# A change of order at the beginning of a perceiver layer: two PSUM copies and one weight transfer

## The chip, the core and the metric

The kernel runs on one core of a Trainium2 chip. The metric is the device time of one execution in microseconds (us), and "the time" of a kernel is the median of its runs. Engines are named as in the profile: PE is TensorE (matmuls; PEld its weight loads), DVE is VectorE, ACT is ScalarE, POOL is GpSimd, and SP is the engine whose queue issues nearly all transfers.

## The reference

One layer of a perceiver. A latent x of 128 rows and 512 columns attends over a context of 12544 rows with 16 heads of 128; then follow a linear attention with decay and a feed-forward part with quantized weights. Nearly all the work is in the first part:

```python
def _L0_xattn_ref(inputs_q, inputs_kv, Wq, Wk, Wv, Wo):
    q = (inputs_q @ Wq).reshape(b, sq, H, HD) * (1.0 / np.sqrt(HD))
    k = (inputs_kv @ Wk).reshape(b, skv, H, HD)
    v = (inputs_kv @ Wv).reshape(b, skv, H, HD)
    scores = jnp.einsum('bqhd,bkhd->bhqk', q, k)
    attn = jax.nn.softmax(scores, axis=-1)
    ctx = jnp.einsum('bhqk,bkhd->bqhd', attn, v).reshape(b, sq, H * HD)
    return ctx @ Wo
...
x = x + _L0_xattn_ref(_layernorm(x, axis=-1), ctx_2048, ...)
x = x + _L0_attn_ref(_layernorm(x, axis=-1), ...)
x = x + _L0_ffn_ref(_layernorm(x, axis=-1), ...)
```

All of it is float32.

## The kernel before

**The algebra.** The kernel never forms the keys. It multiplies each head's query with that head's part of Wk, which gives for 16 heads and 128 rows a matrix of 512 by 2048, and multiplies the context with that matrix to get the scores. The 12544 context rows are taken in 98 pairs of 128; the 2048 score columns in two halves, f = 0 and f = 1. One unit (i, f) is a context pair times a half. Scores go to DRAM; a second pass reads them back, takes the exponential, and multiplies it with the context (L469).

**A unit.** A unit (`unit`, L180) is computed as a block product with seven products instead of eight (p1 to p7), from sums of the context blocks (S1 to S4) and sums of the matrix blocks (T1 to T4). To keep float32 accuracy each operand is split into a high part, a rounding cast made by ScalarE, and a low part, the rest, made by VectorE, and each product is six matmuls of 128x512 (L190), each sum of which lies in one PSUM tile `ps`. ScalarE copies p1 out (L225, `p1s`), VectorE adds the others up (L219: U2, U3, c22, c21, c12), and keeps a running maximum (L237).

**The beginning.** It builds the matrix. The weights of the heads are taken in eight pairs, numbered h2 = 0 to 7 ("the fifth pair" is h2 = 4). For each pair:

- `load_w` (L280) names two transfers of 512 KB, Wq's part (`wq`) and Wk's part (`wk`); `begin` (L298) issues them on SP's queue. `load_ct` (L151) issues a transfer of a context pair, 512 KB too.
- q: `project_q` (L337), 16 matmuls at L344, into a PSUM tile `pq`; needs `wq`.
- qT: `scaled` (L354), ScalarE scales and copies it out (L356).
- k: `project_k` (L358), 16 matmuls at L364, into a PSUM tile `pk` of 128 x 1024 f32; needs qT and `wk`.
- ca and cb: `leave` (L382), two copies by ScalarE of the halves of `pk` into the matrix blocks (L384). Both wait for the whole of k.

The PSUM pool of the beginning, `ps_pro` (L277), has two tiles of each name, so two pairs' `pk` at a time. A third can be written only when both copies of one of them are done.

**The order.** The sums and casts of the matrix blocks stand between these steps: `hB111` is the high part of block B11 for f = 1 (ScalarE, L409), `lB111` its low part (VectorE, L398), `T11` the sum T1 for f = 1 (VectorE, L398), S00 to S23 the sums of the first three context pairs (L163 to L166), `hi0` and `lo0` the split of the first (L171, L176). All of them, and the first four units (u00 to u11, of which `u00p1` is the product p1 of the first), are issued in an order written out by hand in one text, `plan` (L266), and each engine keeps that order for its own instructions. At `u00p1` the pool `ps_pro` is closed and `ps_s`, with eight PSUM tiles, is opened in the same memory; with `reuse_waits="tile"` a tile of it waits only for those old tiles that it lies on. From the third context pair on the order is not written out, but planned by the framework.

**The transfers.** They are issued on SP's queue in this order: x, wq0, wq1, wk0, wk1, wq2, wk2, the first context pair, wq3, wk3 (L304 to L306), then wq4, wk4, the second context pair, and wq5, wk5, wq6, wk6, wq7, wk7 (L331, L333).

Of the kernel before, what the change touches and what calls it, by code (L numbers as in the profile page):

```python
# [33 lines left out]
def tile_perceiver_layer(  # L34
# [116 lines left out]
    def load_ct(i):  # L151
        if i == 1:
            raw = spare(B22, [P, 8, 2, P])
        else:
            raw = ctp.tile([P, 8, 2, P], F32, tag="raw", name="ctr", bufs=1)
        nc.sync.dma_start(out=raw[:, A11:, :, :], in_=cT[i])
        return raw
# [22 lines left out]
    def unit(i, f, place):  # L180
# [83 lines left out]


    plan = """  # L266
        q0 q1 qT0 k0 qT1 k1 c0a c0b q2 c1b hB210 lB210 q3 qT2 c1a hB110 S01 S00 k2 S02 qT3 lB110 S03 k3 c2b c2a hi0
        S11 q4 S10 S12 S13 c3b lo0 ct2 c3a q5 qT4 hB220 T10 k4 qT5 hi1 T30 k5 T20 hT10 lo1 hT30 q6 c4b c5a T40 q7 qT6
        hT20 lB220 c5b k6 lT20 qT7 hT40 lT30 k7 c6a lT40 c6b c4a lT10 u00p1 c7a hB111 u00p6 c7b lB111 hB221 u00p7 T11
        u00p1s u00U2 hT11 u00p5 u00U3 hB211 u00p4 u00c22 T21 u00p2 u00c21 hT21 T31 u00p3 u00c11 lT21 hT31 u10p1 u00c12  # L270
        lT31 u10p6 u10p1s lB221 u10p7 u10U2 u10p5 u10U3 S20 u10p4 u10c22 lB211 u10p2 T41 u10p3 u10c21 hT41 lT11 u10c11
        u01p1 lT41 u01p6 u01p1s u10c12 u00m2 u01p7 u01U2 u01p5 u01U3 S22 u01p4 u01c22 S21 S23 u01p2 u01c21 u10m1 u01p3
        u01c11 u10m2 u11p1 hi2 u01c12 u01m2 u11p6 u11p1s lo2 u11p7 u11U2 u11p5 u11U3 u11p4 u11c22 u11p2 u11c21 u11m1
        u11p3 u11c11 u11c12 u11m2
    """
    pro = ExitStack()
    ps_pro = pro.enter_context(tc.tile_pool(name="ps_pro", bufs=2, space=PSUM))  # L277
# [2 lines left out]
    def load_w(h2):  # L280

        hs = slice(h2 * 256, (h2 + 1) * 256)
        room = {2: B11, 3: B21, 5: T3, 6: T1}
        if h2 in room:
            both = spare(room[h2], [P, 2, 1024])
            wq = both[:, 0, :].rearrange("p (c e) -> p c e", c=NC)
            wk = both[:, 1, :].rearrange("p (h d) -> p h d", h=2)
        else:
            if h2 == 7:
                wq = mxp.tile([P, NC, 256], F32, tag="mx1", name="wq")  # L290
            else:
                wq = ctp.tile([P, NC, 256], F32, tag="hi", name="wq")
            wk = ctp.tile([P, 2, D], F32, tag="lo", name="wk")
        first = [(wq, x_wq[:, hs].rearrange("(c p) e -> p c e", p=P))]
        first.append((wk, x_wkT[hs, :].rearrange("(h p) d -> p h d", p=P)))
        return wq, wk, first

    def begin(*loads):  # L298
        for to, given in loads:
            nc.sync.dma_start(out=to, in_=given)  # L300

    keep_warm(ps_pro, 9)
    ws = [load_w(h2) for h2 in range(4)]
    begin(ws[0][2][0], ws[1][2][0], ws[0][2][1], ws[1][2][1], *ws[2][2])  # L304
    raws[0] = load_ct(0)
    begin(*ws[3][2])  # L306
    xn = mxp.tile([P, D], F32, tag="mx1", name="xn")
    xnT = tmp.tile([P, NC, P], F32, tag="u3", name="xnT")
    st = small.tile([P, 1, 6], F32, tag="bn", name="st")
# [860 lines left out]
```

## Time and profile before

| what | us |
|---|---|
| median of 3 runs | 2129.59 (2127.59 to 2129.66) |
| the profiled execution | 2127.83 |
| its span in the profile | 2126.1 |
| TensorE busy, 0 to 10 | 7.66 |
| 10 to 20 | 9.04 |
| 20 to 30 | 10.00 |
| 30 to 40 | 8.67 |
| 40 to 50 | 9.27 |
| 50 to 2060 | 2010.00 |
| 2060 to 2126 | 58.03 |

The span runs from the first to the last instruction of one execution, and the profiled execution is a little longer than it. Times in a timeline are counted from the span's start. The two big loops (the scores to 973 us, the second pass to 2039 us) keep TensorE busy without a gap, at the full granted clock (1.00 in all stretches); what isn't busy lies in the first 50 us and in the last 66.

The transfers of the beginning, by issue and by landing (us, from the view of the transfers):

| transfer | issued | from issue to landing |
|---|---|---|
| wk2 | 3.87 | 10.2 |
| first context pair | 4.74 | 10.6 |
| wq3 | 5.98 | 10.9 |
| wk3 | 6.75 | 11.4 |
| wq4 | 9.14 | 10.6 |
| wk4 | 12.47 | 8.6 |
| second context pair | 12.89 | 9.5 |
| wq5 | 13.40 | 10.4 |
| wk5 | 14.05 | 11.1 |

### The profile page before, as it was taken

The page shows a single profiled execution, that of the slowest core. Times are in us where ns is not written, and L with a number is a line of the kernel's source. Part 1 is how long each engine was busy: PE and PEld are TensorE (multiplying, and loading weights), DVE is VectorE, ACT ScalarE, POOL GpSimd, SP SyncE. Part 2 cuts the span into 40 slices and gives each one's busy share as a digit, 9 for nine tenths or more (in the row PEclk, how much of TensorE's full clock was granted, in tenths as well). Part 3 has the DMA queues.
Part 4 walks back from the last instruction along what each step waited for, and adds up shares of the span by engine and source line. Part 5 has one row for each costly group of instructions (what it writes and reads, how often), then busy time and mean ns, then how long its engine had stood idle before and what let it go on. Part 6 is the DMA issues. An engine that isn't in the chain of part 4 may idle for free.

```text
span 2126.1 us, 23916 instructions
## 1 busy us (share of the span) xinstructions
PE 2112.7 (99%) x9591; PEld 1745.2 (82%) x9595; DVE 1646.7 (77%) x1827; ACT 754.2 (35%) x846; POOL 25.7 (1%) x15
## 2 busy tenths in 40 slices
PE   8999999999999999999999999999999999999998
PEld 7888888888888888888888888888888888888885
DVE  6877777777777777778897888887788777777745
ACT  6222122211222122214444444444544444444424
POOL 0000000000000000000000000000010000000010
PEclk9999999999999999999999999999999999999999
DMA  5333333333333333336664454553444434444460
GB/s 207 135 140 127 149 141 137 139 129 149 134 144 137 130 149 129 149 151 216 216 238 150 181 179 168 174 202 143 149 149 149 148 142 140 145 142 146 149 230 6
DMA packets 70767, 326.22 MB, mean 153 GB/s; under 512 B 7265, under 2 KB 11617, under 8 KB 45185
## 3 DMA queue, kind: packets, MB, share of 16 engines
q1 hardware_dynamic: 70512, 324.57, 41.4%
q8 instruction: 75, 1.23, 0.2%
q14 instruction: 36, 0.29, 0.1%
q10 hardware_dynamic: 144, 0.13, 0.0%
HBM read 221.65 MB, written 103.02 MB: 153 GB/s over the span
## 4 chain that ended last, share of the span: by engine, by line
PE 98%; DVE 1%; DMA 1%; ACT 0%; SPq 0%; issue 0%; DVEq 0%; ACTq 0%
PE pu L469 50%; PE ps L190 44%; PE pc L742 1%; PE po L763 1%; PE pk L364 1%; DMA kq<-in_x_wq_dram 1%; PE pp L853 0%; PE pq L344 0%; PE po L906 0%; PE pv L876 0%; SPq L300 0%; DVE uT L1057 0%; DVE st L1031 0%; PE pp L932 0%; ACT kq L409 0%
## 5 line engine op out<-in xcount | busy, mean ns | idle before, releaser
L190 PE MATMUL ps<-kq,cth 128*128 128x512 f32 x2744 | 844.5, 389 | 0.0
L469 PE MATMUL pu<-ph,cl 128*128 128x512 f32 x1568 | 610.0, 389 | 0.0
L469 PE MATMUL pu<-pl,ch 128*128 128x512 f32 x1568 | 610.0, 389 | 0.0
L469 PE MATMUL pu<-ph,ch 128*128 128x512 f32 x1568 | 610.0, 389 | 0.0
L190 PEld LDWEIGHTS ps<-kq,cth 128*128 128x128 f32 x2744 | 515.2, 188 | 106.6
L190 PE MATMUL ps<-kq,ctl 128*128 128x512 f32 x1344 | 522.8, 389 | 0.0
L523 ACT CAST ph<-si 128x1024 fp32r<-128x1024 f32 x194 | 203.9, 1051 | 491.9 <-PE pu L469 491.7
L469 PEld LDWEIGHTS pu<-pl,ch 128*128 128x128 f32 x1568 | 294.4, 188 | 61.2
L469 PEld LDWEIGHTS pu<-ph,cl 128*128 128x128 f32 x1568 | 294.4, 188 | 60.9
L469 PEld LDWEIGHTS pu<-ph,ch 128*128 128x128 f32 x1568 | 294.4, 188 | 60.9
L219 DVE TENSOR_TENSOR so<-ps,u 128x512 f32<-128x512 f32 x294 | 202.7, 690 | 134.9 <-PE ps L190 130.5
L190 PEld LDWEIGHTS ps<-kq,ctl 128*128 128x128 f32 x1344 | 252.3, 188 | 52.4
L511 DVE TENSOR_TENSOR cl<-cr,ch 128x1024 fp32r<-128x1024 f32 x98 | 120.2, 1227 | 204.8 <-ACT ch L505 204.8
L254 ACT COPY so<-ps 128x512 f32<-128x512 f32 x98 | 57.6, 588 | 577.6 <-PE ps L190 577.6
L528 DVE TENSOR_TENSOR pl<-si,ph 128x1024 fp32r<-128x1024 f32 x194 | 242.4, 1250 | 1.0 <-ACT ph L523 1.0
L237 DVE TENSOR_TENSOR mx<-mx,so 128x1024 f32<-128x1024 f32 x190 | 232.2, 1222 | 6.7
L517 DVE TENSOR_TENSOR si<-si,mb 128x1024 f32<-128x1024 f32 x194 | 235.7, 1215 | 0.0
L536 DVE TENSOR_TENSOR lsum<-lsum,si 128x1024 f32<-128x1024 f32 x192 | 233.8, 1218 | 0.0
L518 ACT ACTIVATE si<-si 128x1024 f32<-128x1024 f32 x194 | 205.4, 1059 | 60.4 <-DVE si L517 60.4
L505 ACT CAST ch<-cr 128x1024 fp32r<-128x1024 f32 x98 | 102.3, 1044 | 0.0
L176 DVE TENSOR_TENSOR ctl<-ctr,cth 128x1792 fp32r<-128x1792 f32 x47 | 94.9, 2019 | 0.7 <-ACT cth L171 0.7
L171 ACT CAST cth<-ctr 128x1792 fp32r<-128x1792 f32 x48 | 81.7, 1703 | 37.5 <-PE ps L190 35.5
(224 smaller groups left out, 757.8 us busy)
## 6 DMA issues: line engine op xcount, KB each, us to landing
sc<-so SPq DMA_DIRECT2D x98, 1024.0 KB, 3.8
si<-sc SPq DMA_DIRECT2D x97, 1024.0 KB, 5.0
cr<-in_c_dram SPq DMA_DIRECT2D x98, 512.0 KB, 3.5
ctr<-in_cT_dram SPq DMA_DIRECT2D x48, 512.0 KB, 3.5
kq<-in_w1T_dram SPq DMA_DIRECT2D x16, 512.0 KB, 4.3
kq<-in_w2T_dram SPq DMA_DIRECT2D x16, 512.0 KB, 5.0
kq<-in_x_wv_dram SPq DMA_DIRECT2D x3, 1024.0 KB, 5.2
kq<-in_x_wo_dram SPq DMA_DIRECT2D x3, 1024.0 KB, 7.3
```

Source lines behind the costliest of these rows:

```text
L176: return lo, nc.vector.tensor_tensor(lo, raw[:, :7, :, :], hi, ALU.subtract)
L190: nc.tensor.matmul(ps, lhsT=lt[:, a, cc, :], rhs=right(f, b, part)[:, cc, :], start=(first and n == 0), stop=(n == 5), skip_group_check=True,)
L219: place(nc.vector.tensor_tensor(to, t[p], t[q], ALU.add))
L237: place(nc.vector.tensor_tensor(mx[f], mx[f], t["so"][:, j, :], ALU.max))
L469: nc.tensor.matmul(pu[b][cc], lhsT=lt[:, j, cs], rhs=rt[:, bs], start=(first and n == 0), stop=(last and n == 2))
L505: seq(nc.scalar.copy(ctx_hi[f, i], ctx_raw[f, i]))
L511: seq(nc.vector.tensor_tensor(ctx_lo[f, i], ctx_raw[f, i], ctx_hi[f, i], ALU.subtract))
L517: seq(nc.vector.tensor_tensor(exps[k], exps[k], mb[f], ALU.subtract))
L518: seq(nc.scalar.activation(exps[k], exps[k], AF.Exp))
L523: seq(nc.scalar.copy(high[k], exps[k]))
L528: seq(nc.vector.tensor_tensor(low[k], exps[k], high[k], ALU.subtract))
L536: seq(nc.vector.tensor_tensor(lsum[f], lsum[f], exps[k], ALU.add))
```

## The change

It moves three things and adds or removes none.

1. In the plan, `c4a` (the fifth pair's second copy) goes from behind `c6b` to ahead of `c6a`, directly behind `k7`.
2. In the plan, `c7b` (the last copy) goes from behind `hB111 u00p6` to directly behind `c7a`. On ScalarE it passes one cast, `hB111`.
3. `wq3` is issued ahead of the first context pair and not behind it.

All other lines of the plan are the same words in the same order, with other line breaks. The core of the diff:

```diff
-        hT20 lB220 c5b k6 lT20 qT7 hT40 lT30 k7 c6a lT40 c6b c4a lT10 u00p1 c7a hB111 u00p6 c7b lB111 hB221 u00p7 T11
-        u00p1s u00U2 hT11 u00p5 u00U3 hB211 u00p4 u00c22 T21 u00p2 u00c21 hT21 T31 u00p3 u00c11 lT21 hT31 u10p1 u00c12
...
+        T40 q7 qT6 hT20 lB220 c5b k6 lT20 qT7 hT40 lT30 k7 c4a c6a lT40 c6b lT10 u00p1 c7a c7b hB111 u00p6 lB111
+        hB221 u00p7 T11 u00p1s u00U2 hT11 u00p5 u00U3 hB211 u00p4 u00c22 T21 u00p2 u00c21 hT21 T31 u00p3 u00c11
...
     keep_warm(ps_pro, 9)
     ws = [load_w(h2) for h2 in range(4)]
-    begin(ws[0][2][0], ws[1][2][0], ws[0][2][1], ws[1][2][1], *ws[2][2])
+    begin(ws[0][2][0], ws[1][2][0], ws[0][2][1], ws[1][2][1], *ws[2][2], ws[3][2][0])
     raws[0] = load_ct(0)
-    begin(*ws[3][2])
+    begin(ws[3][2][1])
```

More of the change, by code (lines that the diff above doesn't have):

```diff
@@ L266, in tile_perceiver_layer @@
     plan = """
-        q0 q1 qT0 k0 qT1 k1 c0a c0b q2 c1b hB210 lB210 q3 qT2 c1a hB110 S01 S00 k2 S02 qT3 lB110 S03 k3 c2b c2a hi0
-        S11 q4 S10 S12 S13 c3b lo0 ct2 c3a q5 qT4 hB220 T10 k4 qT5 hi1 T30 k5 T20 hT10 lo1 hT30 q6 c4b c5a T40 q7 qT6
-        hT20 lB220 c5b k6 lT20 qT7 hT40 lT30 k7 c6a lT40 c6b c4a lT10 u00p1 c7a hB111 u00p6 c7b lB111 hB221 u00p7 T11
-        u00p1s u00U2 hT11 u00p5 u00U3 hB211 u00p4 u00c22 T21 u00p2 u00c21 hT21 T31 u00p3 u00c11 lT21 hT31 u10p1 u00c12
[L271 to L274, printed above, removed]
+        q0 q1 qT0 k0 qT1 k1 c0a c0b q2 c1b hB210 lB210 q3 qT2 c1a hB110 S01 S00 k2 S02 qT3 lB110 S03 k3 c2b c2a
+        hi0 S11 q4 S10 S12 S13 c3b lo0 ct2 c3a q5 qT4 hB220 T10 k4 qT5 hi1 T30 k5 T20 hT10 lo1 hT30 q6 c4b c5a
+        T40 q7 qT6 hT20 lB220 c5b k6 lT20 qT7 hT40 lT30 k7 c4a c6a lT40 c6b lT10 u00p1 c7a c7b hB111 u00p6 lB111
+        hB221 u00p7 T11 u00p1s u00U2 hT11 u00p5 u00U3 hB211 u00p4 u00c22 T21 u00p2 u00c21 hT21 T31 u00p3 u00c11
+        lT21 hT31 u10p1 u00c12 lT31 u10p6 u10p1s lB221 u10p7 u10U2 u10p5 u10U3 S20 u10p4 u10c22 lB211 u10p2 T41
+        u10p3 u10c21 hT41 lT11 u10c11 u01p1 lT41 u01p6 u01p1s u10c12 u00m2 u01p7 u01U2 u01p5 u01U3 S22 u01p4
+        u01c22 S21 S23 u01p2 u01c21 u10m1 u01p3 u01c11 u10m2 u11p1 hi2 u01c12 u01m2 u11p6 u11p1s lo2 u11p7 u11U2
+        u11p5 u11U3 u11p4 u11c22 u11p2 u11c21 u11m1 u11p3 u11c11 u11c12 u11m2
     """
```

## The prediction

> **What bounds the kernel now.** I read the busy shares first, then the chain of work that ended last, then the waits of TensorE alone, and last the timeline of the first 50 us.
>
> ```profile
> PE 2112.7 (99%) x9591; PEld 1745.2 (82%) x9595; DVE 1646.7 (77%) x1827; ACT 754.2 (35%) x846; POOL 25.7 (1%) x15
> PE 98%; DVE 1%; DMA 1%; ACT 0%; SPq 0%; issue 0%; DVEq 0%; ACTq 0%
> ```
>
> TensorE is busy for 2112.7 of 2126.1 us. So only the 13.4 us in which it stands still can be won, and the table of stretches finds none of them between 50 and 2060 us. The two product lines of the chain run at one rate in both halves (L190: 931.89 us for 4110, 0.2267 each; L469: 1066.24 us for 4704, 0.2267). An edit in the beginning is worth the idle time that it takes from TensorE there, and no more. TensorE's own waits, those of the beginning:
>
> ```profile
> PE pk L364 <- ACT kq L384: 1.2, 1, 1.2
> PE pq L344 <- DMA kq<-in_x_wq_dram: 1.0, 1, 1.0
> PE ps L190 <- ACT kq L384: 0.7, 1, 0.7
> PE pk L364 <- ACT b L384: 0.2, 1, 0.2
> ```
>
> And where they lie (TensorE's timeline, then ScalarE's; start, duration, in brackets the idle time before):
>
> ```profile
> 14.06 1.95 PE L344 MATMUL pq<-xnT,kq 128*128 128x128 f32 x16
> 16.98 2.02 PE L344 MATMUL pq<-xnT,kq 128*128 128x128 f32 x16 [0.96 <-DMA kq<-in_x_wq_dram]
> ...
> 24.20 1.95 PE L344 MATMUL pq<-xnT,kq 128*128 128x128 f32 x16
> ...
> 33.46 2.05 PE L364 MATMUL pk<-qT,kq 128*128 128x128 f32 x16 [0.17 <-ACT b L384]
> 36.67 2.05 PE L364 MATMUL pk<-qT,wk 128*128 128x128 f32 x16 [1.16 <-ACT kq L384]
> ...
> 40.84 0.50 PE L190 MATMUL ps<-kq,mb 128*128 128x512 f32 x1 [0.73 <-ACT kq L384]
> ```
> ```profile
> 33.67 1.04 ACT L409 CAST kq<-b 128x1024 fp32r<-128x1024 f32 x1
> 35.55 1.07 ACT L384 COPY kq<-pk 128x512 f32<-128x512 f32 x2 [0.84 <-PE pk L364]
> 36.51 0.61 ACT L384 COPY b<-pk 128x512 f32<-128x512 f32 x1
> 38.76 0.59 ACT L384 COPY kq<-pk 128x512 f32<-128x512 f32 x1 [1.65 <-PE pk L364]
> 39.24 1.05 ACT L409 CAST kq<-b 128x1024 fp32r<-128x1024 f32 x1
> 40.19 0.59 ACT L384 COPY kq<-pk 128x512 f32<-128x512 f32 x1
> ```
>
> The reader is to see three stalls, one for each of the three edits. q3 (16.98) waits for the transfer of its weights. k7 (36.67) starts 0.05 us after the two copies c6a and c6b end (35.55 + 1.07 = 36.62), while c4a, put behind them, runs from 36.51: so k7 took the place that k6 left, since k4's was held until c4a. u00p6 (40.84) starts 0.06 us after c7b ends (40.19 + 0.59 = 40.78), which stood behind the cast hB111 (39.24).
>
> [...] the transfers of SP's queue landed one after the other, 1.3 to 1.5 us apart, while the stretch from 2 to 30 us moved 360 GB/s at full DMA share. [...] I count landings (issue plus time to landing), not issues.
>
> **The change part by part.**
>
> *The transfer.* Issued at 4.74, the first context pair landed 10.6 us later, at 15.34; wq3, issued at 5.98, landed 10.86 later, at 16.84, so 1.50 after it. Swapped, wq3 lands near 15.4 to 15.6 and the context pair at 16.84; both issues (0.72 and 1.20 us on SP) keep their two places together, and wk3 and all behind it stay. q2 ends at 14.06 + 1.95 = 16.01, so q3 finds its weights there and its 0.96 us of waiting goes. The context pair's first reader is VectorE's sum at 17.10, behind a subtraction that ends at 17.18 whatever happens; 16.84 is 0.26 earlier, so that is hidden. If it came later than that, the four sums would shift by as much, and their reader, the cast at 21.78, still has 2 us behind their end (19.79).
>
> What is late next is wq5. It was issued at 13.40 and took 10.4 us: it lands at 23.80, its place in the queue unchanged. q5 started at 24.20; 0.96 earlier would be 23.24, but it can't start before 23.80 + 0.14 (q3's own distance from landing, 16.98 - 16.84) = 23.94. So of 0.96 us only 24.20 - 23.94 = 0.26 is left. Bounds: 0.1, if starting from rest costs the 0.07 by which q3's group (2.02) is longer than the others (1.95) and a little more; 0.96, if wq5 lands earlier than I think. I take 0.26. wq6 and wq7 landed at 26.7 and 29.55, at least 1.6 us ahead of their matmuls.
>
> *c4a ahead of c6a.* On ScalarE c4a now follows hT40, which ends at 33.67 + 1.04 = 34.71, and fills the 0.84 us in which ScalarE waited for k6; its 0.61 us end at about 35.3, before k6 ends (33.46 + 2.05 = 35.51). k4's place is then free, k7 follows k6 at once, and its 1.16 us go (all these times less the 0.26). Cover: 0.2 us; if it is gone, k7 waits by so much. c6a and c6b start no later than before. Behind them only VectorE's T-sums wait, after 38. Bounds for this edit: 0, if k7 is still given k6's place, and 1.35, the idle time of the weight loads there. I take 1.16.
>
> *c7b ahead of hB111.* Counted from k7's start, c7a comes 2.09 later (38.76 - 36.67), c7b then ends 1.07 after that, as the pair c6a and c6b did: 3.16. u00p1 starts 1.81 after k7 and lasts to about 3.25 (six matmuls, the first at 38.48, the last begun at 39.72). So even if u00p6 lies in k7's banks, c7b is done when its turn comes, and if k7 has moved into k4's banks it waits for nothing: the 0.73 us go. The price is that hB111 is 0.59 us later behind its copies; its reader, a subtraction on VectorE, and T11 behind it then start 1.0 us sooner than before and not 2.15. That is hidden: the first sum that TensorE needs back, c22, follows them and would be at about 43.1, just as its matmuls end (45.21 - 2.15 = 43.06), and TensorE came for it only 1.83 us after its end (45.94 to 47.77).
>
> *Sum.* 0.26 + 1.16 + 0.73 = 2.15 us of the profiled execution: its 2127.83 (a span of 2126.1 and 1.7 around it) becomes 2125.7. The median of the runs shown, 2129.59, lies 1.76 above that execution; the same difference from it gives 2127.4, 0.10% less.
>
> **Rivals.**
> 1. wq5 doesn't bind, and all three stalls go whole: 0.96 + 1.16 + 0.73 = 2.85, so 2126.7. For it: nothing in the trace but the uncertainty of a landing by some tenths; against: the queue is full up to 30 us.
> 2. The second edit does nothing: k7 still takes k6's place. Then 0.26 + 0.73, 2128.6. Against: c4a is over before c6a can begin.
> 3. u00p1 draws one of k7's new banks. Before it didn't wait, so its bank was not among those read by c7a or c7b; k4's pair is not excluded by that, as c4a ended at 37.12. It would then wait from 1.81 to 3.21 after k7's start, 1.40: 2.15 - 1.40 = 0.75 gained, 2128.8.
> 4. Slower than before: from the third context pair on the order is not written out but planned, and a beginning shortened by 2 us could plan VectorE's maxima (1.22 each, L237) ahead of c22. In the loop c22 ended 1.83 us before TensorE came for it (93.54 to 95.37), once only 0.78 (85.07 to 85.85). Two maxima ahead, 2.44, leave a stall of 0.61 in the unit. It decides from the fourth such unit on (2.44 against 2.15 gained); in each second of 192 units it costs 58.6, about 2186. For it: VectorE is busy for 19.03 of 20 us from 60 to 80. Against: every part of the beginning moves by nearly the same 2 us, so the plan's relations stay.
>
> **How the numbers follow.** Chances: forecast 0.60, first rival 0.10, second 0.11, third 0.11, fourth 0.08. The three runs shown spread by 2.07 us, and 0.2% (4.3 us) is about what a measurement of this kernel tells from no change. The forecast and the first rival pass that bound only with some 2 us of luck from the spread, about a quarter of their 0.70: faster 0.18. The fourth is slower: 0.08. The rest, 0.74, stays within. The range goes from 2125.0 (the level of the profiled execution, 2127.83, less the 2.85 of the first rival) to 2129.9 (the third rival and half the spread), which leaves out the fourth and a tenth more.
>
> **What would show it.** After: q3 without idle time; a new wait of 0.5 to 0.8 us of a later q on its weights' transfer near 23.9; k7 right behind k6 near 35.2; u00p1 near 37.0 and u00p6 near 38.5 without idle time; the chain's first long piece of L190 beginning 2.15 earlier, and the products still at 0.2267 us each with no idle time to 2030. I would be wrong if q5 doesn't wait, if k7 still waits for c6b, or if TensorE idles anywhere after 50 us.

## The result, and the profile after

| | median us | runs | range |
|---|---|---|---|
| before | 2129.03 | 22 | 2127.59 to 2129.96 |
| after | 2126.13 | 22 | 2124.84 to 2128.18 |

The ratio is 0.9987, with a 95% interval from 0.9981 to 0.9993: 2.9 us less, and by the interval between 1.5 and 4.0. The forecast was 2127.4 (2.15 less, 0.10%), the range 2125.0 to 2129.9. Of the 1.3 us between forecast and result 0.56 lies in the starting point, for the three runs of before known then had a median of 2129.59, and the rest in the gain. The profiled execution of after took 2127.29 us, with a span of 2125.6; why it lies above the median is shown below.

TensorE's waits in the beginning, after (what waited for what: us in total, times, longest):

```profile
PE pq L344 <- DMA kq<-in_x_wq_dram: 0.9, 1, 0.9
PE pq L344 <- DMA wq<-in_x_wq_dram: 0.9, 1, 0.9
```

The two waits for copies (1.2 and 0.7 before) are no longer in the list. A wait of some q for its weights still is, and a second one has come. TensorE's timeline says which, and ScalarE's what made room (start, duration, in brackets the idle time before):

```profile
14.83 3.74 PE L344 MATMUL pq<-xnT,kq 128*128 128x128 f32 x32
...
24.79 2.02 PE L344 MATMUL pq<-xnT,kq 128*128 128x128 f32 x16 [0.86 <-DMA kq<-in_x_wq_dram]
...
34.12 2.05 PE L364 MATMUL pk<-qT,kq 128*128 128x128 f32 x16 [0.17 <-ACT b L384]
36.01 1.95 PE L364 MATMUL pk<-qT,wk 128*128 128x128 f32 x16
37.72 0.48 PE L190 MATMUL ps<-kq,mb 128*128 128x512 f32 x1
...
39.19 0.39 PE L190 MATMUL ps<-kq,mb 128*128 128x512 f32 x1
...
40.55 0.39 PE L190 MATMUL ps<-kq,mb 128*128 128x512 f32 x1
```
```profile
34.33 1.04 ACT L409 CAST kq<-b 128x1024 fp32r<-128x1024 f32 x1
35.27 0.59 ACT L384 COPY b<-pk 128x512 f32<-128x512 f32 x1
36.21 1.07 ACT L384 COPY kq<-pk 128x512 f32<-128x512 f32 x2 [0.35 <-PE pk L364]
38.00 1.07 ACT L384 COPY kq<-pk 128x512 f32<-128x512 f32 x2 [0.71 <-PE pk L364]
```

q2 and q3 stand in one row of 32 (14.83): q3 waits no more, and q5 (24.79) waits in its stead. k7 (36.01) comes 1.89 us after k6 without idle time, where it came 3.21 after it before; c4a (35.27) is over at 35.86, ahead of k7's start, while c6a and c6b begin only at 36.21, behind it: so k7 can't lie in k6's place. u00p6 (39.19) follows u00p1 without a gap. In the chain of work, told in order of time (start, duration), the two big loops run at their old rate:

```profile
37.96 932.99 PE ps L190 x4116
970.95 1066.24 PE pu L469 x4704
```

That is 0.2267 us per matmul in both, as before, and between 50 and 2030 us TensorE is busy throughout.

**Where the profiled execution lost part of the gain.** All that lies behind the beginning is only 1.77 us earlier than before, and the span 0.5 shorter. Two things explain it. First, the weights came later in this execution: wq5 had landed at 24.65 us, not 23.80, and already q1 waited for wq1 (the second line of the waits). Second, near the end TensorE's granted clock was 0.50 for 3.41 us (from 2110.90 on, in the trace of after), where it stayed at 1.00 before. The table of stretches from 2110 to 2115 us (length; PE busy and matmuls; granted clock; DMA share; GB/s), before and then after:

```profile
2110.00:2115.00 5.00, 3.39 (x10) 1.00 0.00 0
```
```profile
2110.00:2115.00 5.00, 5.00 (x10) 0.66 0.00 0
```

And TensorE's timeline there, before and then after:

```profile
2111.61 2.81 PE L1062 MATMUL pn<-uT,diagonal 128*128 128x512 f32 x6 [2.22 <-DVE uT L1057]
```
```profile
2109.84 4.42 PE L1062 MATMUL pn<-uT,diagonal 128*128 128x512 f32 x6 [2.22 <-DVE uT L1057]
```

The same six matmuls took 4.42 us and not 2.81, and of that 1.25 us reached the end (the lead of 1.77 became 0.52). Without the 0.85 of the later weights the lead would have been 2.62. That is the gain counted from the landing of wq5 to the first matmul of u00p7, the first product behind all three stalls: 42.33 - 23.80 = 18.53 us before, 40.55 - 24.65 = 15.90 after. From it 2127.83 - 2.62 + 0.85 + 1.25 = 2127.31, measured 2127.29; the terms are differences between these two profiles, so the sum says where the time went and is no test of the causes. Those are tested below. The first matmuls of u00p1 and of u00p7 in the profile before:

```profile
38.48 0.48 PE L190 MATMUL ps<-kq,mb 128*128 128x512 f32 x1
...
42.33 0.39 PE L190 MATMUL ps<-kq,mb 128*128 128x512 f32 x1
```

I use this distance below, since it takes out when the transfers came.

### The profile page after: what moved, and what is told of

Same layout as the page of the kernel before. It is cut to its first block, busy times and chain, and to the rows that moved or that the text cites. A ratio compares the mean times of both kernels' runs of the same rounds, so it can differ in the third digit from the quotient of the medians.

```text
span 2125.6 us, 23917 instructions
## 1 busy us (share of the span) xinstructions
PE 2113.8 (99%) x9591; PEld 1745.4 (82%) x9595; DVE 1646.5 (77%) x1827; ACT 754.0 (35%) x846; POOL 25.7 (1%) x15
## 4 chain that ended last, share of the span: by engine, by line
PE 98%; DMA 1%; DVE 1%; ACT 0%; issue 0%; SPq 0%; DVEq 0%; ACTq 0%
PE pu L469 50%; PE ps L190 44%; PE pc L742 1%; PE po L763 1%; DMA kq<-in_x_wq_dram 0%; PE pk L364 0%; DMA wq<-in_x_wq_dram 0%; PE pp L853 0%; PE pq L344 0%; PE pn L1062 0%; PE po L906 0%; PE pv L876 0%; PE pw L92 0%; DVE st L1031 0%; PE pp L932 0%
```

## The experiments

The distance is that from the landing of wq5 to the first matmul of u00p7, from one profile each; the ratio is against runs of the kernel before on the same chip.

| kernel | distance us | median us | ratio and interval |
|---|---|---|---|
| before | 18.53, again 18.50 | 2129.06 | |
| e1 transfer only | 18.35 | 2129.23 | 1.0001 [0.9993, 1.0009] |
| e2 c4a only | 16.10 | 2126.09 | 0.9988 [0.9981, 0.9995] |
| e3 c7b only | 17.56 | 2127.72 | 0.9994 [0.9986, 1.0002] |
| after | 15.90, again 15.89 | 2126.13, again 2126.16 | 0.9987 [0.9981, 0.9993], again 0.9988 [0.9982, 0.9995] |
| e5 wq5 later | 17.54 | 2128.00 | 0.9996 [0.9988, 1.0004] |
| e6 order of transfers | 15.93 | 2125.40 | 0.9983 [0.9977, 0.9990] |
| e7 e6 and c5b | 15.93 | 2124.81 | 0.9982 [0.9974, 0.9990] |
| e8 no gap at the end | 15.91 | 2125.68 | 0.9987 [0.9981, 0.9994] |
| e9 e7 and e8 | not bound by wq5 | 2124.36 | 0.9979 [0.9971, 0.9986] |

The runs of before beside them had medians of 2129.06 (e1 to e3), 2128.51 (e5 to e8) and 2128.86 (e9, after again). The totals alone can't part neighbours, for their intervals reach 1.3 to 1.7 us to each side; the distance and the named waits can.

**The kernel before, once more** (the same text).

> The kernel before, a second profile. If the landings of the first transfers differ from one execution to the next whatever the order, wq1 lands elsewhere than at 8.50 us (after: 9.26) and q3 waits for wq3 until it has landed plus 0.14. If the later landings were brought by the change, wq1 lands at 8.5 again. And if the halved clock at the end of the profile of after is a matter of the single execution, the six matmuls of L1062 take 2.8 or 4.4 us here without regard to the beginning.

wq1 landed at 8.47, wq5 at 24.01, q3 waited 1.18 us, and the six matmuls took 2.8 us. So the landings differ by some tenths between executions of one kernel, and q3's wait with them; the distance is the same within 0.03.

**One part at a time.** First the transfer:

```diff
-    begin(ws[0][2][0], ws[1][2][0], ws[0][2][1], ws[1][2][1], *ws[2][2])
+    begin(ws[0][2][0], ws[1][2][0], ws[0][2][1], ws[1][2][1], *ws[2][2], ws[3][2][0])
     raws[0] = load_ct(0)
-    begin(*ws[3][2])
+    begin(ws[3][2][1])
```

> Only wq3 ahead of the first context pair. Theory: the wait moves from q3 to q5, which then starts 0.14 us after wq5 lands; 0.1 to 0.4 us less, ratio 0.9998 to 1.0000. k7 (1.16) and u00p6 (0.73) wait as before. Rival (the wait goes whole): q5 doesn't wait, 0.96 us less, ratio 0.9995.

TensorE's timeline of this kernel:

```profile
24.23 2.02 PE L344 MATMUL pq<-xnT,kq 128*128 128x128 f32 x16 [0.78 <-DMA kq<-in_x_wq_dram]
...
36.78 2.05 PE L364 MATMUL pk<-qT,wk 128*128 128x128 f32 x16 [1.16 <-ACT kq L384]
...
40.94 0.50 PE L190 MATMUL ps<-kq,mb 128*128 128x512 f32 x1 [0.71 <-ACT kq L384]
```

wq5 landed at 24.09 and q5 started at 24.23, 0.14 us later, as counted. The stall has moved, and 18.50 less 18.35 is what is left of it: 0.15 to 0.18 us. The total doesn't show it (11 of its 13 runs had the lower mean clock of which the last section tells).

Then the first of the two copies alone:

```diff
-        ... lT30 k7 c6a lT40 c6b c4a lT10 u00p1 ...
+        ... lT30 k7 c4a c6a lT40 c6b lT10 u00p1 ...
```

> Only c4a ahead of c6a. Theory: k7 takes the place of k4, its 1.16 us of idle time go, and since u00p6 lies in the place that k7 had before, where c6b is now the last reader, its 0.73 go as well although c7b still stands behind hB111; about 1.9 us less, ratio 0.9991. q3 waits as before. Rival (u00p6 waits for c7b wherever k7 lies): u00p6 stands still for 0.8 to 1.1 us until c7b ends, and only 0.9 to 1.2 us are gained, ratio 0.9995.

TensorE's timeline, and ScalarE's:

```profile
33.96 2.05 PE L364 MATMUL pk<-qT,kq 128*128 128x128 f32 x16 [0.17 <-ACT b L384]
35.85 1.95 PE L364 MATMUL pk<-qT,wk 128*128 128x128 f32 x16
37.56 0.47 PE L190 MATMUL ps<-kq,mb 128*128 128x512 f32 x1
...
39.02 0.40 PE L190 MATMUL ps<-kq,mb 128*128 128x512 f32 x1
...
40.40 0.39 PE L190 MATMUL ps<-kq,mb 128*128 128x512 f32 x1
```
```profile
38.32 1.05 ACT L409 CAST kq<-b 128x1024 fp32r<-128x1024 f32 x1
39.27 0.59 ACT L384 COPY kq<-pk 128x512 f32<-128x512 f32 x1
```

u00p6 starts at 39.02 without idle time, and c7b, still behind the cast, begins only at 39.27. So u00p6 doesn't wait for c7b as such: it waits for the last reader of the places that it lies on (the prediction's banks), and with k7 in k4's places that reader is c6b, long done (c6a and c6b ended at 37.12). Which places a tile got is not in the trace; it follows from these starts. This one edit takes both stalls, 18.5 to 16.10, 2.4 us, and its time is that of the whole change.

Then the other copy alone:

```diff
-        ... u00p1 c7a hB111 u00p6 c7b lB111 ...
+        ... u00p1 c7a c7b hB111 u00p6 lB111 ...
```

> Only c7b ahead of hB111. Both theories: k7 waits for c6b as before (1.16), u00p6 doesn't wait any more (0.73), 0.7 to 0.9 us less, ratio 0.9996. q3 waits as before. If u00p6 still waits, what it waits for is not c7b.

```profile
37.16 2.05 PE L364 MATMUL pk<-qT,wk 128*128 128x128 f32 x16 [1.16 <-ACT kq L384]
...
40.44 0.44 PE L190 MATMUL ps<-kq,mb 128*128 128x512 f32 x1
```

In TensorE's timeline k7 waits as before, and u00p6 doesn't. The distance is 0.95 us shorter. So c7b's edit works alone; but 2.42 for c4a and 0.17 for the transfer make 2.59 of the 2.62 of the whole, which leaves 0.03 for c7b beside c4a. The times agree when runs with the same mean granted clock are compared, which is 1.000 in some runs and 0.999 in the others (why is in the last section). With 1.000 the medians are 2128.11 before, 2127.16 with c7b alone (0.95 less), 2125.49 with c4a alone (2.62 less) and 2125.60 with all three (2.51 less).

**Is q5's wait the bound now?** The kernel after, with the two transfers of the sixth pair exchanged:

```diff
-        begin(*ws[h2][2])
+        begin(*(ws[h2][2][::-1] if h2 == 5 else ws[h2][2]))
```

> The kernel after, with wq5 issued behind wk5 and not ahead of it (the wait that I hold to be the new bound, lengthened). Theory: wq5 lands one transfer later, 1.36 us, q5 waits by that much longer (0.86 becomes 2.2) and the end moves by the same 1.3 us: 1.3 less of the gain, ratio 0.9993. Rival (q5's wait is hidden by something behind it): the end moves by less than 0.4 us.

TensorE's timeline, and then the table of stretches:

```profile
25.16 3.15 PE L344 MATMUL pq<-xnT,kq 128*128 128x128 f32 x16 [2.32 <-DMA kq<-in_x_wq_dram]
```
```profile
24.00:26.00 2.00, 0.84 (x7) 0.95 1.08 364
26.00:28.00 2.00, 2.00 (x11) 0.50 1.09 365
28.00:30.00 2.00, 2.00 (x15) 0.69 1.03 383
```

The wait grew by 1.46 us over the 0.86 of after, and the median by 1.9: nothing behind q5 hides its wait. In this profile the granted clock also fell to 0.50 behind the long gap (0.95, 0.50 and 0.69 in the three stretches, together some 3.4 us at half clock from about 25.8 on). By an estimate from these lengths that is worth 1.7 us, half of 3.4; without it the distance is 17.54 - 1.70 = 15.84, that of after. Among runs with a mean clock of 1.000 the medians are 2127.30 here (5 runs) and 2125.60 for after, 1.7 apart. That is 0.2 more than the wait grew, which stays open.

**Taking the bound away.** The kernel after, with the second context pair and wq5 issued ahead of wk4, which has more time (in the kernels with this edit the line numbers behind it are three higher, since it adds three lines):

```diff
-    for h2 in range(4, 8):
+    ws.append(load_w(4))
+    begin(ws[4][2][0])
+    raws[1] = load_ct(1)
+    ws.append(load_w(5))
+    begin(ws[5][2][0], ws[4][2][1], ws[5][2][1])
+    for h2 in range(6, 8):
         ws.append(load_w(h2))
         begin(*ws[h2][2])
-        if h2 == 4:
-            raws[1] = load_ct(1)
```

> The kernel after, with the second context pair and wq5 issued right behind wq4, ahead of wk4. wk4 then lands about 2.8 us later, near 23.8 to 24.6, and k4 needs it from 25.0 on. Theory: q5 doesn't wait any more, 0.8 to 1.1 us less than after, the first product of the first unit starts 0.8 to 1.1 us sooner after the landing of wk3; ratio 0.9983. Rival (the next thing in line takes it back): k4 waits for wk4, or k6 for the casts behind the sums, and under 0.4 us are gained.

The median is 0.7 us below that of after, but the profiled execution still shows q5 waiting:

```profile
24.80 2.02 PE L347 MATMUL pq<-xnT,kq 128*128 128x128 f32 x16 [0.84 <-DMA kq<-in_x_wq_dram]
```

wq5 landed at 24.66, no earlier than in after (24.65, with wk3 at 18.98 there and 19.01 here), although one transfer fewer lay ahead of it. What the landings show of it is in the last section. So the theory came near for the times (0.7 of the expected 0.8 to 1.1) and failed for this execution.

With c5b moved ahead of a cast as well:

```diff
-        ... q7 qT6 hT20 lB220 c5b k6 ...
+        ... q7 qT6 c5b hT20 lB220 k6 ...
```

> As e6_pair_and_wq5_ahead, and c5b ahead of the cast hT20, so that k6 needn't wait for it. Theory: k6's 0.17 us (0.36 for its weight loads) go, 0.2 to 0.4 us less than e6; k7 may wait for c4a by 0 to 0.3, since c4a stays behind hT40. Rival: hT20 and hT40 come later by the copy (0.59) and c4a with them, and nothing is gained.

```profile
23.50 2.02 PE L347 MATMUL pq<-xnT,kq 128*128 128x128 f32 x16 [0.35 <-DMA kq<-in_x_wq_dram]
...
34.65 2.05 PE L367 MATMUL pk<-qT,wk 128*128 128x128 f32 x16 [0.17 <-ACT b L387]
```

Here the rival was right: k6's 0.17 us are gone, and k7 waits 0.17 for c4a, which now comes later by the copy. The distance is that of e6, 15.93. The lower median doesn't show otherwise: over the runs with a granted clock of 1.000 alone the medians are 2124.42 for this kernel and 2124.31 for e6.

**The halved clock at the end.** The kernel after, with more matmuls of zeros, which `keep_warm` issues, in the gap of 2.22 us:

```diff
-    keep_warm(ps_w, 12)
+    keep_warm(ps_w, 21)
```

> The kernel after, with 21 and not 12 matmuls of zeros ahead of the six matmuls of L1062, so that TensorE's gap of 2.22 us there shrinks to about 0.3. Theory: the halved clock comes from that gap [...]; without it no execution shows 0.999, the six matmuls take 2.8 us in all of them, the fastest runs are as fast as those of after (2124.8) and the slower ones (2126.5 to 2128.2) go: a median 0.3 to 0.7 us lower. Rival: the halving has nothing to do with the gap, and a third of the runs still shows 0.999.

The gap went to 0.28 us. 3 of 21 runs had a mean clock below 1.000, where after had 8 of 22 (and 11 of 21 when it was measured again), and the median is 0.45 lower. So the gap is most of the cause and not all of it. The three are not profiled; in this kernel q5 still waits, 1.68 us in its profile, and in e5 the clock fell to 0.50 behind a wait of 2.32 us at that place too.

**All together**, e7 and e8:

> e7_and_sixth_copy with the 21 matmuls of zeros of e8_no_gap_at_end. Theory: the two gains add, since one is in the first 50 us and the other in the last 20: a median of 2124.2 to 2124.6, ratio 0.9980, and at most one run in seven below a granted clock of 1.000. Rival: e7's gain was the luck of its share of full clocks, and the median is no lower than that of e8 (2125.7).

Its timeline, the beginning and the end:

```profile
23.36 1.95 PE L347 MATMUL pq<-xnT,kq 128*128 128x128 f32 x16
...
39.07 0.39 PE L190 MATMUL ps<-kq,mb 128*128 128x512 f32 x1
...
2108.35 2.81 PE L1065 MATMUL pn<-uT,diagonal 128*128 128x512 f32 x6 [0.27 <-DVE uT L1060]
```

In this profile q5 no longer waits (39.07 is the first matmul of u00p7), and all 16 runs had a clock of 1.000. At 2124.36, ratio 0.9979 [0.9971, 0.9986], it is the fastest here, 1.8 us below after.

**The kernel after, once more** (the same text).

> The kernel after, a second profile and time. Theory: a median near 2126.1, ratio 0.9987; q5 starts 0.14 us after wq5 lands, wherever that landing falls (23.8 to 24.7 in the executions seen so far), and the first product after the stalls starts 15.8 to 16.0 us after that landing. Rival: q5's wait in the first profile was chance, and here it is under 0.3 us.

wq5 landed at 23.93, q5 started at 24.07 after a wait of 1.14, u00p7 15.89 after the landing: as the theory has it. The median is 2.70 us below that of before beside it.

## Why the prediction was right, and where its terms were off

The mechanism was right in its main steps, and the waits show it. The median alone would not: at 2126.13 it lies nearer to the first rival (2126.7) than to the forecast (2127.4), and the range had room for all but the fourth.

- *What can be won.* Right: only idle time of TensorE in the beginning was won; the loops kept their rate and there is no idle time from 50 to 2060 us. That rules out the fourth rival.
- *The transfer.* The step held in each part: wq5, whose landing was estimated to stay at 23.80 when two transfers ahead of it change places, landed at 24.09 in e1 and at 23.80 and 24.01 in the two profiles of before; q3's wait goes, q5 is late next, 0.14 us behind wq5. The term was put at 0.26 and measured 0.15 to 0.18: q5, which now starts from rest, took 2.02 us and not 1.95, a cost that the prediction named in its bounds and left out of its sum. The first rival (nothing binds behind it) falls: q5 waited 0.78 to 1.14 in the profiles of e1 and after.
- *c4a.* Right that k7 would get k4's place, and the second rival (k7 still takes k6's) falls, since k7 started ahead of c6a; that it took k6's before was read from the two start times alone. The term 1.16 was too small. From the start of k6 to that of u00p1 the time fell from 5.02 us (33.46 to 38.48) to 3.60 (33.96 to 37.56 in e2): 1.42. The idle time of the matmul row leaves out what starting from rest costs; the range named 1.35, the idle time of the weight loads, and that was nearer.
- *c7b.* The 0.73 was gained, but it was booked to the wrong edit. The prediction said itself that u00p6 waits for nothing if k7 has moved, and still gave the sum's third term to c7b. The runs show that c4a takes it (e2), that c7b takes it alone (e3), and that together they take it once. The sum stood all the same, since all three edits were made. The size of this term is 1.0: from u00p1 to u00p7 3.85 us became 2.84.
- *The sum.* 0.26 + 1.16 + 0.73 = 2.15 was forecast. 0.17 + 1.42 + 1.01 = 2.60 was measured by these parts, 2.62 as a whole, and 2.9 in the medians, whose interval holds both; the second measurement of after gave 2.70.
- *The cover.* c22 started at 44.04, where 43.1 had been counted and the weights came 0.85 later, and no product waited for it. The third rival (u00p1 on k7's banks) falls: u00p1 started with no idle time.

## What to carry to other kernels

Here a wait for a buffer was a wait for the last reader of the place that was handed out, and not for the copy that happened to end just then (in e2 u00p6 started at 39.02 and c7b at 39.27); one copy moved changed who got which place and ended two stalls at once (2.4 us), so that the edits aimed at each didn't add up (2.42 and 0.95 alone, with the transfer's 0.17, against 2.62 together). Ask first which place a tile was given and who reads it last. Count a stall from start to start of the work on both sides of it, since idle time alone was 18 and 28% too small here (1.16 for 1.42, 0.73 for 1.01). When a wait for a transfer goes, look up the landing of the next one in the same queue first: here it took back five sixths of the 0.96 us.

## What the runs showed of the hardware

**Half clock after a short gap.** In the trace of after the granted clock was 0.50 for 3.41 us, from 2110.90 on, 1.06 us after TensorE had gone on behind its gap of 2.22 us (L1062). In e5 it was 0.50 for about 3.4 us, from some 0.6 us behind the end of the gap of 2.32 us. The profile of before has the same gap of 2.22 us, and the clock behind it was 1.00. The mean clocks of the profiled executions were 0.999 in after, e1, e2, e3, e5 and e7, and 1.000 in before, its second profile, the second of after, e6, e8 and e9, while TensorE's wait at L1062 was 2.2 us in e1, e2 and e3 as in before. So a gap of 2.2 us was followed by the half clock in some executions and not in others, and what decides is not shown. The mean clock was below 1.000 in 68 of 134 runs of before and in 19 of 43 of after, in 3 of 21 with the gap at 0.28 us (e8) and in none of 16 of e9.

In the profiled execution of after that stretch and another at 0.50 in the last 1.0 us of its span of 2125.6 us make a mean clock of 0.999; that of before, at 1.00 to the end of its span, had 1.000. The difference makes a good part of the spread: among the runs of after the median is 2125.60 with a mean clock of 1.000 (14 runs) and 2126.88 below it (8), among those of before that ran beside e1 to e3 2128.11 (18) and 2129.51 (23). Compared within a clock, the change is worth 2.5 to 2.6 us, and in the second measurement of after 2.5 to 2.7.

**A landing is the last of sixteen counts.** In the traces each transfer's semaphore gets sixteen counts, and the landing is the time of the last. In the profile of after the last came 2.13 us behind the fifteenth at wq1's landing (9.26), still 1.65 behind at wq4's (20.47) and 0.69 behind at wq5's (24.65); in that of before it came 0.62, 0.35 and 0.21 behind at the same three (8.50, 19.69 and 23.80). At wq5 the fourteenth came at 22.92 in after and at 23.38 in before, 0.46 earlier, so the 0.85 us by which wq5 landed later lie in the last two counts alone. A packet of 16 KB of the instruction queue started at 20.28 us in after and at 20.56 in before, and took 1.1 us in both. In after the fifteenth count came 0.21 us behind the fourteenth at wq4's landing (20.47) and 0.98 behind at the second context pair's (23.15); in before it stayed at 0.2 (at 21.05, 22.36 and 23.80). So it is not shown that the packet is the cause. Whatever the cause, moving a transfer ahead by one place, put at 1.4 us from landings that lie 1.3 to 1.5 us apart in before, brought nothing in the profiled execution of e6: wq5 landed at 24.66, and at 24.65 in after.
